# Eight-head attention that sums its second exponentials on TensorE, taps and evictions moved to ScalarE, and strands ranked by arrival

## The chip, the cores and the metric

The kernel runs on one core of one Trainium2 chip. The metric is the device time of one execution in microseconds (us); the time before is the median of three executions. A core has five engines with a queue of their own each: TensorE (PE, matmuls, with its weight loads shown apart as PEld), VectorE (DVE), ScalarE (ACT), GpSimd (POOL) and SyncE (SP), which here only issues DMA transfers. Matmul results land in PSUM, eight banks of 128 partitions by 512 float32; everything else is in SBUF or in device memory.

## The reference

Eight images of 256 channels by 32 x 32 points (N = 1024 positions) go through four layers. Only the parts that matter here are shown.

```
layer 0   four-head attention + 3x3 depthwise position term, then a gated feed-forward:
          1x1 conv to 1024 channels, 3x3 depthwise conv, gelu(x1) * x2, 1x1 conv, 8x8 FFT filter
layer 1   xn = group_norm(x)
          q, k, v = 8 heads of 32 channels from one 1x1 conv
          attn = softmax(q^T k * temperature, over keys)       # 1024 x 1024 for each head
          out = v attn^T ;  x = x + w_out out + b_out ;  then a small MLP
layer 2   quantized bottleneck: 1x1, 3x3, 1x1 conv
layer 3   Mamba over four scan orders: in-projection, causal conv of 4 taps + SiLU, selective scan
          with 16 states, gate, out-projection
```

## The kernel before, in words

The program has two phases, one after the other on the same core.

`phase_a` holds layers 0 to 2 and the in-projection and causal conv of layer 3 (`mix`). `phase_b` holds the selective scan. The change touches `phase_a` alone.

In `phase_a` the work of each image is written as a Python generator, a strand, that yields instructions. `sample(b)` runs `layer0`, `feed_forward`, `layer1`, `layer2` for image `b` and then adds the strand `mix(b)`. Image `b` may begin when image `b - 3` is through layer 0, so some three images are on their way at once. A planner, the class `_Order`, writes the instructions out: it keeps a planned time for each engine and buffer from fixed costs in `_Op`, and emits next the strand whose next instruction can start earliest; ties go to the lower rank, a pair of (class, image), and among equal ranks to the strand that was added first. So the order on every engine is fixed when the program is built. The planner also fills gaps on TensorE with dummy matmuls of a constant (`keep_dense`, line 302), where less than half of its last 3.4 us was dense work in its own plan.

Buffers are rooms of numbered tiles. PSUM is the room `bank` with 8 banks. While an attention runs (`attending` is a lock, one attention at a time), all other strands together may hold `OTHERS` = 3 banks; the attention holds one accumulator `po` and takes 4 banks for each step of scores.

Attention goes over the scores twice:

- `maxima` (line 620): for each of 8 position tiles, 2 key halves and 4 heads it makes a 128 x 512 block of scores, VectorE takes its maximum (`tensor_reduce`, 128 x 512 from PSUM), and ScalarE makes the exponentials of that block with `accum_out`, the sum along the row. The bank goes back after that. From maxima and sums a short chain of small operations makes the logarithm of the softmax denominator, which is written as three bfloat16 terms in rows (`parts`, `rows`). `MAXIMA` is the number of strands that share one such list.
- `exponentials` (line 686): for each key tile it makes four transposed blocks of scores, adds minus those rows by a bfloat16 matmul, takes the exponentials on ScalarE (`exps`), and multiplies them with v on TensorE into `po` (`values`). Since the rows hold the whole log-denominator, the result is already normalised; `finish` only copies `po` out.

One image has 64 blocks of maxima and 16 steps in layer 0, and 128 blocks (two groups of four heads) and 32 steps in layer 1. In layer 1 a `finish` ends 8 steps, four times for each image.

Other places that the change touches: the first tap of the depthwise conv in `feed_forward` (`chunk`, 8 of 128 x 1024 for each image, VectorE), the eviction of `k` in `layer1` (4 of 128 x 512 for each image, VectorE), and in `mix` the eviction of the in-projection (8 of 128 x 512, VectorE) and the first tap with its bias of the causal conv (16 of 128 x 1024, VectorE; the other three taps follow on VectorE, then SiLU on ScalarE). `mixing` is a lock: one image is mixed at a time.

Nearly all instructions are emitted by one helper, so the profile puts them on line 154; tiles tell them apart.

Of the kernel before, what the change touches and what calls it, by code (L numbers as in the profile page):

```python
# [344 lines left out]
def phase_a(ctx, tc, i, col, ident, codes, w_parts, mixes):  # L345
# [20 lines left out]
    OTHERS = 3  # L366
    MAXIMA, SCORES = 1, 1.29
    GATE = 1
# [5 lines left out]
    mixing = []  # L374
    RANK = lambda b: (2, b)
    stats = _Room(rooms, "stats", 3, [P, 2, 2, NT, 4])
# [30 lines left out]
    mean = const("mean", [P, P], 1.0 / C)  # L407
    minus = const("minus", [P, P], -1.0, BF16)
    eps0 = const("eps0", [P, 1], 1e-6)
    parts = const("parts", [P, NT, 4, 32], 0.0)  # L410
# [208 lines left out]

    def maxima(rank, q, k, rows, done):  # L620

        both = yield from take(stats)
        least, sums = both[:, 0], both[:, 1]
        todo = [(t, j, h) for t in range(NT) for j in range(2) for h in range(4)]
        left = [MAXIMA]

        def some():
            while todo:
                yield lambda: not todo or may(min(3, len(todo)))
                if not todo:  # L630
                    break
                n = min(len(todo), 4)
                while not may(n):
                    n -= 1
                n = min(n, 4)
                take_now, todo[:n] = todo[:n], []
                bb = yield from some_banks(n)
                ops = []
                for b, (t, j, h) in zip(bb, take_now):
                    r = slice(32 * h, 32 * h + 32)  # L640
                    ops.append(T.matmul(b, lhsT=q[r, t * P : (t + 1) * P], rhs=k[r, hs(j)], start=True, stop=True))
                yield (0.96 if n > 2 else 1.06, ops)
                for b, (t, j, h) in zip(bb, take_now):
                    m, s = (x[:, j, t, h : h + 1] for x in (least, sums))
                    yield V.tensor_reduce(m, b, AX.X, ALU.max, negate=True)
                    yield A.activation(b, b, AF.Exp, bias=m, accum_out=s)
                    back(b)
            left[0] -= 1

        for _ in range(MAXIMA):  # L650
            order.add((1, rank), some())
        yield lambda: left[0] == 0 and not making
        making.append(1)
        m, mx, t = (small.tile([P, NT, 4], F32, name=f"mx{e}", tag=f"mx{e}", bufs=2) for e in range(3))
        yield V.tensor_tensor(m, least[:, 0], least[:, 1], ALU.min)
        for j in range(2):
            yield V.tensor_tensor(least[:, j], m, least[:, j], ALU.subtract)
        yield A.activation(least, least, AF.Exp)
        yield V.tensor_tensor(sums, sums, least, ALU.mult)
        yield V.tensor_tensor(t, sums[:, 0], sums[:, 1], ALU.add)  # L660

        y = small.tile([P, NT, 4], F32, name="ln", tag="ln", bufs=2)
        put(stats, both)
        yield A.activation(y, t, AF.Ln)
        yield V.tensor_tensor(mx, y, m, ALU.subtract)
        yield A.activation(y, y, AF.Exp, scale=-1.0)
        yield V.tensor_tensor(t, t, y, ALU.mult)
        yield V.scalar_tensor_tensor(mx, t, -1.0, mx, ALU.add, ALU.add)
        for e in range(2):
            b = small.tile([P, NT, 4], BF16, name="mb", tag="mb", bufs=2)  # L670
            yield V.tensor_copy(b, mx)
            yield V.tensor_copy(parts[:, :, :, e], b)
            yield V.tensor_tensor(mx, mx, parts[:, :, :, e], ALU.subtract)
        yield V.tensor_copy(parts[:, :, :, 2], mx)
        for h in range(2):
            pr = yield from side()
            yield [
                T.transpose(pr[:, t * P : (t + 1) * P], parts[:, 4 * h + t].rearrange("p a b -> p (a b)"), ident)
                for t in range(4)
            ]  # L680
            yield A.copy(rows[:, hs(h)], pr)
            back(pr)
        making.clear()
        done()

    def exponentials(rank, tasks, vt, n, finish):

# [4 lines left out]
        for task, (h, steps) in enumerate(tasks):  # L692
            po = yield from take(bank)
            seen = [0]

# [27 lines left out]

            def values(k, four, tiles, po=po, seen=seen, last=len(steps) - 1):
                es = [t[:, e] for t in tiles for e in range(2)]
                yield lambda: seen[0] == k
                ops = []
                for e, (q, kk, rows, key, r, c, at) in zip(es, four):
# [5 lines left out]
                    )  # L734
                yield (0.88 * (4 * n // P) + 0.12, ops)
                for t in tiles:
                    put(exps, t)
# [4 lines left out]
            yield lambda: seen[0] == len(steps)  # L742
            order.add((0, rank), finish(task, po))
        attending.clear()
# [17 lines left out]
    def layer0(b, x):  # L762
        rank = b
        xn = yield from rms(x, "n1w", "n1b")
# [47 lines left out]

        def finish(task, po):
            h, p = divmod(task, 2)
# [52 lines left out]
    def feed_forward(b, x):  # L867


        rank = b  # L870
        xn = yield from rms(x, "n2w", "n2b")
# [8 lines left out]
        def chunk(o):  # L880
# [19 lines left out]

            yield V.tensor_scalar(acc, hx, w(4), None, ALU.mult)
            for k, dy, dx in _taps():
# [80 lines left out]
    def layer1(b, x):  # L983
        rank = b
        xn = yield from group_norm(x, "g1", "be1")
# [7 lines left out]
        for cc in range(CC):  # L993
            for n in range(2):
                ws.append((yield from weights("w_qkv1", CC * n + cc)))
            for n, dst in enumerate((q, k)):
                w = ws.pop(0)
                for h in range(2):
                    ps = yield from side()
                    yield mm(ps, w, 0, P, xn, h)  # L1000
                    if n == 0:
                        yield A.activation(dst[:, cc, hs(h)], ps, AF.Identity, scale=temp[:, cc : cc + 1])
                    else:
                        yield V.tensor_copy(dst[:, cc, hs(h)], ps)
                    back(ps)
                put(wr, w)
# [3 lines left out]

            order.add((1, rank), maxima(rank, q[:, cc], k[:, cc], rows[cc], done))
        for cc in range(CC):
# [12 lines left out]
        for g in range(CC):  # L1025

            def finish(h, po, g=g):
                yield A.copy(o[:, g, hs(h)], po)
                put(bank, po)
                summed[0] += 1  # L1030

# [7 lines left out]
            yield lambda g=g: ready[g]  # L1039
            yield from exponentials(rank, [(h, steps) for h in range(2)], vt, HD1, finish)  # L1040
            put(low, rows[g])
# [122 lines left out]
    def mix(b):  # L1164


        def branch(c, k, src, back, left):
# [4 lines left out]

            yield V.tensor_scalar(o, src, col("cv_w", 4 * c + PAD), col("cv_b", c), ALU.mult, ALU.add)
            for tap in range(PAD):
# [15 lines left out]
        def chunk(c):  # L1190
# [5 lines left out]
            for h in range(2):  # L1196
# [7 lines left out]
                put(low, xc)  # L1204
                yield V.tensor_scalar(xi[:, hs(h)], ps, col("s3"), None, ALU.mult)
                back(ps)
# [36 lines left out]
    with tc.manual_schedule():  # L1243
        for b in range(B):
            order.add((2, b), sample(b))
        order.add((9, B), weight_parts())
# [604 lines left out]
```

## Time and profile before

| | |
|---|---|
| median of 3 executions | 9355.51 us (9354.29 to 9357.71) |
| profiled execution, its own time | 9359.27 us |
| its span in the profile | 9357.5 us |
| granted TensorE clock, mean | 0.98 |
| last write of `mix`, end of the work of `phase_a` | about 3773 us |
| first scan of `phase_b` | 3807 us |

The span is the time from the first to the last instruction of the program in the profiled execution. Busy time of an engine is the time in which one of its instructions is shown as running; for TensorE the ends are modelled, so that a matmul that is held up by a bank counts as busy. A group is all instructions of one operation on tiles of one name.

### The profile page before, as it was taken

To read this page: it belongs to the slowest core of one execution; us is meant where nothing else is said; L and a number is where in the kernel's file an instruction comes from. 1 tells how busy PE (TensorE), PEld (TensorE's weight loads), DVE (VectorE), ACT (ScalarE), POOL (GpSimd) and SP (SyncE) were. 2 spreads that over 40 slices of the span, in tenths; PEclk is the share of its full clock that TensorE was granted. 3 is DMA by queue.
4 is the path that set the end of the run, shared out by engine and by line. 5 is a ranking of instruction groups with operands and counts; after the bars stand their busy time and mean duration, and the time that the engine had idled before them with its cause. 6 is when DMAs were issued, how large, how long until landed. Compare 5 with 4: busy or idle time off the path is not lost.

```text
span 9357.5 us, 152821 instructions
## 1 busy us (share of the span) xinstructions
PE 8721.1 (93%) x56752; PEld 5778.5 (62%) x56752; DVE 8236.6 (88%) x9134; ACT 7996.2 (85%) x15039; POOL 5674.9 (61%) x2742
## 2 busy tenths in 40 slices
PE   9999999999999998799999999999999999999998
PEld 3333333333333333688788788778788788787787
DVE  7688587969899777899999999999999999999898
ACT  7768576767777774899999999999999999999998
POOL 0010010101111100799999999999999999999999
PEclk9999999999999999999999999999999999999999
DMA  1100111111111112222222212212222222222221
GB/s 57 38 25 22 38 55 49 48 35 49 34 64 57 39 52 85 76 64 66 69 65 66 73 61 65 73 61 67 71 62 68 69 67 65 68 67 64 69 66 58
DMA packets 297420, 548.41 MB, mean 59 GB/s; under 512 B 31761, under 2 KB 98705, under 8 KB 291554
## 3 DMA queue, kind: packets, MB, share of 16 engines
q1 hardware_dynamic: 296674, 538.64, 17.8%
q8 instruction: 446, 7.31, 0.3%
q14 instruction: 300, 2.46, 0.1%
HBM read 427.90 MB, written 100.14 MB: 56 GB/s over the span
## 4 chain that ended last, share of the span: by engine, by line
ACT 24%; PE 24%; DVE 16%; issue 3%; POOL 1%; DMA 0%; DVEq 0%; SPq 0%; POOLq 0%; ACTq 0%
ACT da L154 11%; DVE h L154 11%; ACT dbu L154 9%; PE db L154 8%; PE py L154 7%; PE pp L154 5%; PE bank L154 3%; DVE mx L154 1%; DVE mid L154 1%; DVE stats L154 1%; DVE ys L154 1%; ACT dt L154 1%; ACT L154 1%; DVE yT L154 1%; ACT st L154 1%
## 5 line engine op out<-in xcount | busy, mean ns | idle before, releaser
L154 POOL TENSOR_TENSOR h<-h,cb 128x1024 f32<-128x1024 f32 x2048 | 4798.5, 2388 | 144.2 <-ACT st L154 79.8
L154 ACT ACTIVATE da<-dt,am 128x512 f32<-128x512 f32 x4096 | 2867.8, 714 | 138.5 <-DVE h L154 130.7
L154 DVE TENSOR_TENSOR_SCAN h<-da,db 128x512 f32<-128x512 f32 x2048 | 2330.3, 1199 | 227.9 <-PE db L154 132.2
L154 DVE TENSOR_TENSOR_SCAN h<-da,st,db 128x512 f32<-128x512 f32 x2048 | 2444.0, 1258 | 68.1 <-PE db L154 47.3
L154 ACT ACTIVATE dbu<-du,bT 128x512 f32<-128x512 f32 x3584 | 2476.9, 708 | 9.3 <-PE db L154 5.0
L154 PE MATMUL db<-ident,dbu 128*128 128x128 f32 x14336 | 2134.6, 277 | 316.0 <-DVE h L154 303.6
L154 PE MATMUL py<-ident,h 128*128 128x128 f32 x16384 | 2121.5, 273 | 10.4 <-POOL h L154 6.5
L154 PEld LDWEIGHTS db<-ident,dbu 128*128 128x128 f32 x14336 | 1614.4, 141 | 748.0 <-DVE h L154 486.2
L154 PEld LDWEIGHTS py<-ident,h 128*128 128x128 f32 x16384 | 1849.9, 140 | 29.9 <-POOL h L154 10.6
L154 ACT ACTIVATE bank<-bank,stats 128x512 f32<-128x512 f32 x1536 | 1018.8, 676 | 369.8 <-DVE stats L154 362.8
L154 DVE TENSOR_REDUCE stats<-bank 128x1 f32<-128x512 f32 x1536 | 976.4, 680 | 222.0 <-PE bank L154 218.0
L154 ACT ACTIVATE exps<-bank 128x512 f32<-128x512 f32 x1536 | 793.8, 612 | 194.7 <-PE bank L154 189.6
L154 PE MATMUL bank<-big,big 32*128 32x512 f32 x4096 | 873.8, 659 | 40.7 <-ACT bank L154 18.2
L154 DVE SCALAR_TENSOR_TENSOR mid<-mid,cols,mid 128x961 f32<-128x961 f32 (+2 forms) x560 | 726.0, 1296 | 12.5
L154 POOL COPY mx<-mx 128x1024 f32<-128x1024 f32 x28 | 64.4, 2301 | 903.6 <-DMA mix<-mx 534.9
L154 PEld LDWEIGHTS bank<-big,big 32*128 32x128 f32 x4096 | 297.5, 190 | 480.0 <-issue 209.9
L302 PE MATMUL bank<-minus 128*128 128x512 bf16 x1994 | 522.5, 404 | 37.7 <-ACT exps L154 17.5
L154 PE MATMUL db<-dg,du 128*128 128x128 f32 x4096 | 530.4, 279 | 17.0 <-DVE h L154 16.1
L154 PE MATMUL bank<-exps,big 128*32 128x512 f32 (+1 forms) x3072 | 538.7, 611 | 0.0
L154 POOL TENSOR_TENSOR mid<-mid,mid 128x512 f32<-128x512 f32 x64 | 102.6, 1623 | 689.8 <-DVE mid L154 630.4
L154 PEld LDWEIGHTS db<-dg,du 128*128 128x128 f32 x4096 | 488.7, 192 | 49.3 <-DVE h L154 26.3
L302 PEld LDWEIGHTS <-minus 128*128 128x128 bf16 x2080 | 197.4, 102 | 491.9 <-issue 294.3
(204 smaller groups left out, 9271.5 us busy)
## 6 DMA issues: line engine op xcount, KB each, us to landing
cb<-c_d SPq DMA_DIRECT2D x1024, 256.0 KB, 3.2
xs<-mix SPq DMA_DIRECT2D x256, 256.0 KB, 4.3
mix<-mx SPq DMA_DIRECT2D x112, 512.0 KB, 3.0
big<-in_x_dram SPq DMA_DIRECT2D x16, 1024.0 KB, 5.3
kept<-big SPq DMA_DIRECT2D x16, 1024.0 KB, 5.2
big<-kept SPq DMA_DIRECT2D x16, 1024.0 KB, 6.9
low<-codes SPq DMA_DIRECT2D x64, 256.0 KB, 3.7
wi<-w_in SPq DMA_DIRECT2D x64, 192.0 KB, 3.4
```

The lines of the kernel that those rows point to most:

```text
L154: return getattr(getattr(nc, self.engine), self.method)(*self.args, **self.kw)
L302: self.nc.tensor.matmul(x, lhsT=self.minus, rhs=rhs, start=True, stop=True)
```

## The change

1. In layer 1, `maxima` is called with `shift=True`: VectorE takes the maxima of the blocks as before, but the exponentials with their sums and the chain that makes the logarithm are left out; the three bfloat16 rows hold the maximum alone. Layer 0 stays as it is.
2. In layer 1, `exponentials` is called with `shifted=True`: it takes a second accumulator bank `pz` and adds to each step four more matmuls, a 128 x 32 block of ones against the same exponentials, so that `pz` holds the denominators. `finish` takes the reciprocal of `pz` on VectorE (128 x 512), multiplies `po` by it on VectorE, and gives both banks back; the copy on ScalarE is gone.
3. The first tap of `feed_forward`'s depthwise conv, the first tap of `mix`'s causal conv, the eviction of `k`, and the eviction of the in-projection go from VectorE to ScalarE.
4. `MAXIMA` goes from 1 to 2, and the image leaves the ranks: all images have rank 0, so that ties go to the strand that was added first.

```diff
-    MAXIMA, SCORES = 1, 1.29
+    MAXIMA, SCORES = 2, 1.29
...
-    RANK = lambda b: (2, b)
+    RANK = lambda b: (2, 0)
...
+    ones = const("ones", [P, HD0], 1.0)
...
-    def maxima(rank, q, k, rows, done):
+    def maxima(rank, q, k, rows, done, shift=False):
...
-                    yield V.tensor_reduce(m, b, AX.X, ALU.max, negate=True)
-                    yield A.activation(b, b, AF.Exp, bias=m, accum_out=s)
+                    yield V.tensor_reduce(m, b, AX.X, ALU.max, negate=not shift)
+                    if not shift:
+                        yield A.activation(b, b, AF.Exp, bias=m, accum_out=s)
                     back(b)
...
+        if shift:
+            yield V.tensor_tensor(mx, least[:, 0], least[:, 1], ALU.max)
+            put(stats, both)
+        else:
+            yield V.tensor_tensor(m, least[:, 0], least[:, 1], ALU.min)
...
+            yield V.scalar_tensor_tensor(mx, t, -1.0, mx, ALU.add, ALU.add)
...
-    def exponentials(rank, tasks, vt, n, finish):
+    def exponentials(rank, tasks, vt, n, finish, shifted=False):
...
             po = yield from take(bank)
+            pz = (yield from take(bank)) if shifted else None
...
+                if shifted:
+                    ops = [
+                        T.matmul(
+                            pz[at : at + n], lhsT=ones[:, :n], rhs=e,
+                            start=(k == 0 and key == 0), stop=(k == last), skip_group_check=True,
+                        )
+                        for e, (_, _, _, key, _, _, at) in zip(es, four)
+                    ]
+                    yield (0.88 * (4 * n // P) + 0.12, ops)
...
-            yield V.tensor_scalar(acc, hx, w(4), None, ALU.mult)
+            yield A.activation(acc, hx, AF.Identity, scale=w(4))
...
-                        yield V.tensor_copy(dst[:, cc, hs(h)], ps)
+                        yield A.copy(dst[:, cc, hs(h)], ps)
...
-            def finish(h, po, g=g):
-                yield A.copy(o[:, g, hs(h)], po)
+            def finish(h, po, pz, g=g):
+                t = yield from take(low)
+                yield V.reciprocal(t, pz)
+                put(bank, pz)
+                yield V.tensor_tensor(o[:, g, hs(h)], po, t, ALU.mult)
                 put(bank, po)
+                put(low, t)
...
-            yield V.tensor_scalar(o, src, col("cv_w", 4 * c + PAD), col("cv_b", c), ALU.mult, ALU.add)
+            yield A.activation(o, src, AF.Identity, scale=col("cv_w", 4 * c + PAD), bias=col("cv_b", c))
...
-                yield V.tensor_scalar(xi[:, hs(h)], ps, col("s3"), None, ALU.mult)
+                yield A.activation(xi[:, hs(h)], ps, AF.Identity, scale=col("s3"))
...
-            order.add((2, b), sample(b))
+            order.add((2, 0), sample(b))
```

`rank = b` becomes `rank = 0` in `layer0`, `feed_forward` and `layer1` as well.

More of the change, by code (lines that the diff above doesn't have):

```diff
@@ L654, in maxima @@
         m, mx, t = (small.tile([P, NT, 4], F32, name=f"mx{e}", tag=f"mx{e}", bufs=2) for e in range(3))
[L655 to L668, printed above, removed]
+        if shift:
[3 more added lines that the diff above has]
+            yield V.tensor_tensor(m, least[:, 0], least[:, 1], ALU.min)
+            for j in range(2):
+                yield V.tensor_tensor(least[:, j], m, least[:, j], ALU.subtract)
+            yield A.activation(least, least, AF.Exp)
+            yield V.tensor_tensor(sums, sums, least, ALU.mult)
+            yield V.tensor_tensor(t, sums[:, 0], sums[:, 1], ALU.add)
+            y = small.tile([P, NT, 4], F32, name="ln", tag="ln", bufs=2)
+            put(stats, both)
+            yield A.activation(y, t, AF.Ln)
+            yield V.tensor_tensor(mx, y, m, ALU.subtract)
+            yield A.activation(y, y, AF.Exp, scale=-1.0)
+            yield V.tensor_tensor(t, t, y, ALU.mult)
+            yield V.scalar_tensor_tensor(mx, t, -1.0, mx, ALU.add, ALU.add)
         for e in range(2):
@@ L722, in step, with values @@
                 order.add((1, rank), values(k, four, tiles))
-            def values(k, four, tiles, po=po, seen=seen, last=len(steps) - 1):
+            def values(k, four, tiles, po=po, pz=pz, seen=seen, last=len(steps) - 1):
                 es = [t[:, e] for t in tiles for e in range(2)]
@@ L742, in exponentials @@
             yield lambda: seen[0] == len(steps)
-            order.add((0, rank), finish(task, po))
+            order.add((0, rank), finish(task, po, pz))
         attending.clear()
@@ L762, in layer0 @@
     def layer0(b, x):
-        rank = b
+        rank = 0
         xn = yield from rms(x, "n1w", "n1b")
@@ L811, in layer0, with finish @@
         summed = [0]
-        def finish(task, po):
+        def finish(task, po, pz):
             h, p = divmod(task, 2)
@@ L867, in feed_forward @@
     def feed_forward(b, x):
-        rank = b
+        rank = 0
         xn = yield from rms(x, "n2w", "n2b")
@@ L983, in layer1 @@
     def layer1(b, x):
-        rank = b
+        rank = 0
         xn = yield from group_norm(x, "g1", "be1")
@@ L1009, in done @@
                 ready[cc] = 1
-            order.add((1, rank), maxima(rank, q[:, cc], k[:, cc], rows[cc], done))
+            order.add((1, rank), maxima(rank, q[:, cc], k[:, cc], rows[cc], done, True))
         for cc in range(CC):
@@ L1039, in layer1 @@
             yield lambda g=g: ready[g]
-            yield from exponentials(rank, [(h, steps) for h in range(2)], vt, HD1, finish)
+            yield from exponentials(rank, [(h, steps) for h in range(2)], vt, HD1, finish, True)
             put(low, rows[g])
```

## The prediction

> **What bounds the kernel now.** I read the page first (engine shares and the slices), then busy time by stretches, the groups by shape, and the waits.
>
> ```profile
> PE 8721.1 (93%) x56752; PEld 5778.5 (62%) x56752; DVE 8236.6 (88%) x9134; ACT 7996.2 (85%) x15039; POOL 5674.9 (61%) x2742
> ...
> PE   9999999999999998799999999999999999999998
> ...
> DVE  7688587969899777899999999999999999999898
> ACT  7768576767777774899999999999999999999998
> ```
>
> The slices show two programs: up to slice 16 VectorE and ScalarE change between 4 and 9, after it all are full. The change touches only the first, `phase_a`, which ends at about 3773 us. Its busy times (columns: stretch, its length, then PE, PEld, DVE, ACT, POOL busy, clock, DMA share, GB/s):
>
> ```profile
> 0.00:3773.00 3773.00, 3513.92 (x16346) 1321.74 (x16346) 2998.82 (x4141) 2662.56 (x5707) 359.91 (x236) 0.95 0.14 47
> 3773.00:9357.50 5584.50, 5207.21 (x40406) 4456.71 (x40406) 5237.77 (x4993) 5333.60 (x9333) 5315.04 (x2506) 1.00 0.21 66
> ```
>
> So the second stretch, 5584.5 us, stays. In the first VectorE is busy 79%, ScalarE 71%, TensorE 93%, but that 93% holds dummies and matmuls held up at a bank. No engine bounds all of it; stretches of 100 us tell which bounds where:
>
> ```profile
> 900.00:1000.00 100.00, 97.20 (x693) 31.85 (x694) 27.14 (x55) 83.80 (x182) 2.52 (x2) 0.97 0.00 1
> ...
> 1100.00:1200.00 100.00, 92.45 (x312) 34.59 (x310) 98.66 (x134) 84.84 (x194) 5.52 (x2) 0.91 0.15 56
> ...
> 1900.00:2000.00 100.00, 98.93 (x554) 44.68 (x549) 48.86 (x97) 76.28 (x183) 3.03 (x4) 1.00 0.00 1
> ```
>
> and the same stretches for the dummies of line 302 alone:
>
> ```profile
> 900.00:1000.00 100.00, 1.38 (x4) 0.97 0.00 1
> ...
> 1100.00:1200.00 100.00, 18.70 (x67) 0.91 0.15 56
> ...
> 1900.00:2000.00 100.00, 0.78 (x2) 1.00 0.00 1
> ```
>
> Two kinds. In 14 of the 38 stretches VectorE is above 90% (1100 is one) and TensorE has up to 27 us of dummies to give: VectorE bounds. In six others (300, 600, 900, 1400, 1900, 3200) there are at most 8 dummies and TensorE is at 94 to 100%: mostly attention, where TensorE bounds. ScalarE is never the fullest of the three in either kind.
>
> The rows that price the change:
>
> ```profile
> L154 ACT ACTIVATE bank<-bank,stats 128x512 f32<-128x512 f32 x1536 | 1018.8, 676 | 369.8 <-DVE stats L154 362.8 <-DVE rs L154 3.1 <-ACT bank L154 0.2
> ...
> L154 ACT ACTIVATION_READ_ACCUMULATOR bank<-bank,stats 128x1 f32 x1536 | 333.2, 217 | 0.0
> ```
>
> ```profile
> L154 PE MATMUL bank<-exps,big 128*32 128x512 f32 x2048 | 288.6, 611 | 0.0
> ```
>
> ```profile
> L154 DVE TENSOR_SCALAR mx<-mx,cols 128x1024 f32<-128x1024 f32 x112 | 92.5, 826 | 20.9 <-POOL mx L154 19.2 <-issue 0.4
> ...
> L154 DVE TENSOR_SCALAR mid<-mid,cols 128x1024 f32<-128x1024 f32 x96 | 82.5, 859 | 37.7 <-ACT mid L154 34.4 <-POOL mid L154 2.7
> ```
>
> ```profile
> PEld bank L154 <- ACT bank L154: 262.0, 400, 5.3
> ...
> PEld bank L154 <- ACT exps L154: 135.4, 282, 2.4
> ```
>
> The first two say what one block of first-pass exponentials costs ScalarE; the third prices the new matmuls (same shape, same 1024 instructions, two records each); then the moved taps; the last two how long TensorE's weight loads waited for banks held by first-pass and by second-pass exponentials.
>
> **The change part by part.**
>
> *Load moved.* ScalarE loses 1024 of 1536 blocks at 0.88 us (1018.8 + 333.2 over 1536), 901 us, and some 12 us of the small chain. It gains 64 first taps of the depthwise conv at 1.05 to 1.27 us (the 128x1024 rows without and with two scalar columns, 1049 and 1271 ns), 75; 128 first taps of `mix` at 1.27, 163; 64 evictions at 0.69, 44; 32 copies of `k` replace 32 copies of `po`. Net -631: 2032 us left, 54%. That covers all it gains, and the saved ScalarE time by itself is worth nothing, since ScalarE bounded no stretch. If the cover were gone, it would be 282 us of new work.
>
> VectorE loses 92.5 (112 taps), 69 (80 of the 96 `mid` taps at 0.859), 41.7 + 5.8 (64 evictions), 21.8 (`k`), and 27 of the small chain: 257. It gains 32 multiplies at 0.69, 22, and 32 reciprocals.
>
> *The reciprocal* has one row, 128x7 at the very start:
>
> ```profile
> 2.81 0.70 DVE L154 TENSOR_SCALAR rs<-cols 128x8 f32<-128x8 f32 x1 [2.81 <-DMA cols<-in_cols_dram]
> ...
> 2.96 0.56 DVE L458 RECIPROCAL rq<-cols 128x7 f32<-128x7 f32 x1
> 3.58 0.45 DVE L481 TENSOR_SCALAR sq<-cols,rq 128x1 f32<-128x1 f32 x2
> ```
>
> The instruction two before it ends at 3.51 and its reader begins at 3.58. At the most 0.07 us are its own, 10 ns an element, 5.1 us for 512. At the least it costs what VectorE's 128x512 copy from PSUM does, 0.69. Dependent small operations here follow each other after some 0.03 us; less that, and less the two elements between, about 0.03 us for 7 remain, 4 ns an element. I take 2.2 us: 32 of them 70 us, between 22 and 163.
>
> The Trainium skill speaks against the change here: "VectorE: DVE Perf Modes", section "First, the fixed hardware budget", says that the reciprocal is an iterative divide with a repeat count of 8. At its 0.96 GHz that is an estimated 4.3 us for 512 elements; the one row neither confirms nor excludes it. By the page 32 times 2.1 us come on top, of which 27% and half of the rest count (steps 1 and 4): 42 us, and the sum would end at about 9308 us.
>
> *Step 1, VectorE-bound stretches.* By the start times of the rows, 56% of `mix`'s taps, 46% of the `mid` taps, 59% of the evictions and 56% of the `k` copies lie in the 14 stretches: 52 + 32 + 28 + 12, and 12 of the small chain, 136 us. Of layer 1's 256 steps 27% lie there; of the new 92 us that puts 25 back. Net -111. Next late there is TensorE, whose 91 to 99% hold dummies. The three later taps now wait for ScalarE; behind them in VectorE's queue stands what the planner has put there, and in the 14 stretches other strands fill it. I take 0; the present waits of VectorE for `mid` from ScalarE are 34.4 us in 7 times, so up to 34.
>
> *Step 2, banks of the first pass.* A layer 1 bank goes back after the maximum instead of after 0.88 us more on ScalarE. Two thirds of the 262.0 us are layer 1's, 175; 56% of the maxima lie outside the 14 stretches: -98 (bounds 0 and -175). Next late is the maximum itself, 0.68 us a block.
>
> *Step 3, sums on TensorE.* 256 steps get four matmuls more, side by side in column groups: measured from each start to the next one's they take 272 us in all, 1.06 a step. 88 steps lie in the six stretches without dummies: +93. The other 168 (179 us) are covered by dummies and VectorE-bound time; the built order has 1174 dummies where there were 1994, 215 us less at 0.262. If that cover is gone, the 179 come on top.
>
> *Step 4, ends of groups.* `finish` holds two banks for 2.2 + 0.69 us where a copy took 0.59: 2.3 later, 32 times, 74 us. The next group's accumulators wait for them, other strands do not; 73% lie outside the 14 stretches, half of that on the path: +27 (0 to 130).
>
> *Step 5, one bank less.* Accumulators and four score banks leave 2 banks instead of 3. Layer 1's share of the waits for second-pass exponentials is two thirds of 135.4, 90 us, 0.35 a step; the new 1.06 a step lies over it. I take 0, up to +90.
>
> *Step 6, two maxima strands, order by arrival, the end.* No row shows these. Two strands could take at the best layer 0's third of the bank waits, -87; an image's `mix` that slips past the last image's layer 2 costs 16 branches, 76 us. The built order has 108 of 128 `mix` writes before the last image's last code write, 112 before: four branches more at the end, some 3.9 us each on VectorE, against 0.8 saved on each of 16 or more. +16 and -13: I take 0. SP issues as many DMAs as before; GpSimd gets three instructions more.
>
> *Sum.* -111 - 98 + 93 + 27 = -89, on the profiled execution's 9359.3: 9270. That execution is 4 above the median of the runs, so 9355.5 - 89 = **9266 us**.
>
> **The rivals.**
> 1. *TensorE becomes the bound (slower).* For it: 93% busy and +272. Against: 820 dummies fewer. It costs the 179 us of step 3: -89 + 179 = +90, 9446. It decides once more than 89 of the 179 are uncovered.
> 2. *All overlaps as well as now.* Busy sums are 2999 + 2663 + 3514 = 9176 in 3773, 2.43 engines at once. After: 2834 + 2032 + 3571 = 8437, over 2.43 is 3469: -300, 9055. For it: three fuller engines come nearer to each other. Against: TensorE's share of it cannot shrink to less than its busy 3571.
> 3. *Step 2 is hidden anyway.* For it: ScalarE itself waited 362.8 us for maxima, so the maximum, not the exponential, is late. Then -89 + 98 = +9, 9365, no change that can be told; with half of it, 9315.
>
> **How the numbers follow.** Chances: forecast 0.42 (9200 to 9335), rival 1 0.24, rival 2 or most of the way to it 0.18, rival 3 0.16, of which 0.09 is within 0.2% (19 us, about what this measurement tells from no change), 0.05 above and 0.02 below it. Faster 0.42 + 0.18 + 0.02 = 0.62; same 0.09; slower 0.24 + 0.05 = 0.29. The range leaves out the far part of rivals 1 and 2 and the bounds that would have to fall together: 9140 to 9440; the forecast's own is 9200 to 9335.
>
> **What would show it.** First tap groups of VectorE gone and its stretches above 90% fewer; `PEld bank <- ACT bank` near 90; a `bank<-exps,ones` group near 290 us; the 128x512 reciprocal's mean (above 4 us step 4 and step 1 are too good). The first codes write of the last image and the end of `mix` give each step's sum. The prediction is wrong if TensorE is at 97% or more throughout `phase_a`, or if `phase_b` is not 5584 us.

## The result and the profile after

The changed kernel takes 9336.66 us (median of 17 runs, 9326.52 to 9352.71) where the kernel before takes 9362.99 us in the same comparison (17 runs, 9354.29 to 9370.69). The ratio is 0.9974, with a 95% interval of 0.9966 to 0.9981: 26 us faster, where the forecast was 89. The profiled execution took 9336.66 us.

The page of the changed kernel, engine totals and slices:

```profile
PE 8742.0 (94%) x57896; PEld 5762.6 (62%) x57980; DVE 8141.6 (87%) x8796; ACT 7539.9 (81%) x13201; POOL 5691.1 (61%) x2745
...
DVE  7587688877878976899999999999999999999898
ACT  8774376564445546899999999999999999999998
```

The slices of `phase_a` (up to slice 16) show where work went: in nine of the 16 slices ScalarE's digits fell, in seven of them from 7 to 4 or 5; VectorE's are nearly what they were. The two stretches, cut where the last row of `mix` is written (3751.1 us; it was 3773.1):

```profile
0.00:3754.00 3754.00, 3536.88 (x17535) 1305.58 (x17574) 2903.72 (x3803) 2207.32 (x3871) 378.74 (x240) 0.96 0.14 47
3754.00:9334.90 5580.90, 5205.12 (x40361) 4456.99 (x40406) 5237.86 (x4993) 5332.57 (x9331) 5312.34 (x2506) 1.00 0.23 66
```

From the first scan to the end it is 5549.6 us (5550.5 before): `phase_b` is untouched, and all of the difference lies in `phase_a`. There ScalarE is 455 us less busy, VectorE only 95 less and TensorE 23 more. The groups by shape that the change made or moved:

```profile
L302 PE MATMUL bank<-minus 128*128 128x512 bf16 x1174 | 325.7, 410 | 23.9 <-DVE low L154 7.9 <-DVE big L154 5.3 <-ACT low L154 3.1
...
L154 PE MATMUL bank<-exps,ones 128*32 128x512 f32 x2048 | 288.3, 601 | 0.0
...
L154 DVE SCALAR_TENSOR_TENSOR mx<-mx,cols,mx 128x1021 f32<-128x1021 f32 x112 | 144.6, 1292 | 124.3 <-ACT mx L154 124.3
...
L154 ACT ACTIVATE mx<-mx,cols 128x1024 f32<-128x1024 f32 x112 | 136.4, 1246 | 10.2 <-POOL mx L154 9.3
...
L154 DVE RECIPROCAL low<-bank 128x512 f32<-128x512 f32 x32 | 107.3, 3354 | 82.6 <-PE bank L154 77.5 <-issue 3.7 <-POOL big L154 1.4
```

The new matmuls have the price that was forecast. The reciprocal takes 3.35 us. The second tap of `mix` (third line) now idles VectorE for 124.3 us because ScalarE has not made the first tap yet; before, the first tap stood on VectorE itself and no such wait existed. The waits of `phase_a` (engine, what it waited for, then us in total, times, longest):

```profile
ACT big L154 <- PE bank L154: 377.1, 157, 7.7
...
PEld bank L154 <- ACT exps L154: 162.7, 304, 3.0
DVE mx L154 <- ACT mx L154: 124.3, 19, 13.0
PEld bank L154 <- DVE stats L154: 96.9, 174, 3.0
PEld bank L154 <- ACT bank L154: 71.4, 108, 1.7
...
PEld bank L154 <- DVE low L154: 50.2, 29, 5.1
...
PE bank L154 <- DVE low L154: 35.2, 20, 4.3
```

The wait of weight loads for `ACT bank` fell from 262.0 to 71.4, but 96.9 for the maximum (`DVE stats`, 9.7 before) stand in its place. The last two lines are TensorE waiting for VectorE's writes of `low`, nearly all of them the reciprocal, whose end frees a group's second bank. A weight load and its matmul can wait at the same moment; with such time counted once, the two lines are 57 us of idle time, 6 before. ScalarE's idle time is no loss; the first line (135.7 before) says that it now waits for TensorE.

### The profile page after: what moved, and what is told of

Read it like the earlier page. It is cut to its first block, busy times and chain, and to the rows that moved or that the text cites. A ratio compares the mean times of both kernels' runs of the same rounds, so it can differ in the third digit from the quotient of the medians.

```text
span 9334.9 us, 152169 instructions
## 1 busy us (share of the span) xinstructions
PE 8742.0 (94%) x57896; PEld 5762.6 (62%) x57980; DVE 8141.6 (87%) x8796; ACT 7539.9 (81%) x13201; POOL 5691.1 (61%) x2745
## 4 chain that ended last, share of the span: by engine, by line
PE 39%; ACT 26%; DVE 26%; issue 4%; POOL 1%; DMA 0%; DVEq 0%; SPq 0%; POOLq 0%; ACTq 0%
PE bank L154 18%; ACT da L154 12%; DVE h L154 11%; ACT dbu L154 10%; PE db L154 8%; PE py L154 7%; PE pp L154 5%; DVE stats L154 4%; DVE mid L154 4%; DVE mx L154 2%; DVE low L154 1%; DVE big L154 1%; PE bank L302 1%; DVE ys L154 1%; ACT L154 1%
## 5 line engine op out<-in xcount | busy, mean ns | idle before, releaser
L154 DVE TENSOR_REDUCE stats<-bank 128x1 f32<-128x512 f32 x1536 | 952.0, 680 | 198.1 <-PE bank L154 194.6
L154 PE MATMUL bank<-big,big 32*128 32x512 f32 x4096 | 812.1, 662 | 36.6 <-DVE low L154 25.4
L154 PE MATMUL bank<-exps,big 128*32 128x512 f32 (+1 forms) x3072 | 560.7, 620 | 1.0 <-ACT exps L154 1.0
L154 DVE SCALAR_TENSOR_TENSOR mx<-mx,cols,mx 128x1021 f32<-128x1021 f32 x336 | 441.4, 1323 | 130.3 <-ACT mx L154 124.3
L154 ACT ACTIVATE bank<-bank,stats 128x512 f32<-128x512 f32 x512 | 340.2, 687 | 164.8 <-DVE stats L154 163.3
L154 PE MATMUL bank<-big,wr 128*128 128x512 f32 x896 | 450.6, 632 | 13.2 <-POOL big L154 2.9
```

What stands on the lines that cost most here:

```text
L154: return getattr(getattr(nc, self.engine), self.method)(*self.args, **self.kw)
```

## The experiments

Times are medians, ratios are to the kernel before with the 95% interval, and differences in us are between medians. Two kinds of edit must be kept apart. Where the planner sees other work or other costs, it writes a **new order** for all of `phase_a`. Where an order is **held**, the planner plans the kernel as it was, and only the instruction that is emitted differs.

### Parts with a plan of their own

**The attention change alone**: the changed kernel with everything else as before (one strand, ranks by image, the taps and evictions on VectorE).

```diff
-    MAXIMA, SCORES = 2, 1.29
+    MAXIMA, SCORES = 1, 1.29
-    RANK = lambda b: (2, 0)
+    RANK = lambda b: (2, b)
-            yield A.activation(acc, hx, AF.Identity, scale=w(4))
+            yield V.tensor_scalar(acc, hx, w(4), None, ALU.mult)
...
```

> The attention change alone (sums by products of ones, maximum alone in the rows, reciprocal in finish) on the kernel before: taps and evictions stay on VectorE, one maxima strand, image ranks. Theory T (TensorE takes back most of what the banks give): -10 to +60 us against before, since +93 to +272 us of TensorE work meet -98 us of bank waits and VectorE loses only its 27 us of small chain. Theory R (only the slow reciprocal, 32 x 3.35 us, spoils it): -30 to -90 us. Theory O (the new order and ranks spoil it): -60 to -150 us, since the order parts are left out here.

Measured 9550.63 us, ratio 1.0195 (1.0181 to 1.0210): 187 us slower. ScalarE, relieved, waits for TensorE instead: for its exponentials 463.2 us (189.6 before), for `big` 416.3 (135.7 before). The new sums with the reciprocal are no gain by themselves. Which of their costs makes up the 187 no run separates.

**The rest without the attention change**: the changed kernel with layer 1's sums and evictions of `po` as before.

```diff
-            order.add((1, rank), maxima(rank, q[:, cc], k[:, cc], rows[cc], done, True))
+            order.add((1, rank), maxima(rank, q[:, cc], k[:, cc], rows[cc], done))
...
-                yield V.reciprocal(t, pz)
-                put(bank, pz)
-                yield V.tensor_tensor(o[:, g, hs(h)], po, t, ALU.mult)
+                yield A.copy(o[:, g, hs(h)], po)
...
```

> Taps and evictions on ScalarE, two maxima strands, ranks by arrival; the eight-head attention as before. Theory T: -60 to -110 us against before, the relief of the VectorE-bound stretches without the new TensorE work, so faster than the whole change. Theory R: -80 to -120 us. Theory O: 0 to +60 us. If ScalarE, which here keeps its 901 us of first-pass exponentials and gains 282 us, becomes the bound: 0 to +50 us.

9292.75 us, 0.9926 (0.9913 to 0.9938): 44 us faster than the changed kernel, with all of its ScalarE work back. Alone, the two parts are 187 slower and 71 faster; together they are 26 faster. Parts that each get a plan of their own do not add up.

**The taps and evictions alone**: the kernel before with these lines of the changed one.

```diff
-            yield V.tensor_scalar(acc, hx, w(4), None, ALU.mult)
+            yield A.activation(acc, hx, AF.Identity, scale=w(4))
...
-                        yield V.tensor_copy(dst[:, cc, hs(h)], ps)
+                        yield A.copy(dst[:, cc, hs(h)], ps)
...
```

> The kernel before with the taps and evictions on ScalarE alone: attention, one maxima strand and image ranks as before. The taps, the evictions and the order together gave -71 us. Theory W (the relief of VectorE is what pays): -50 to -120 us against before. Theory O (the order pays, the taps only move work to a ScalarE that is full there): 0 to +60 us.

9347.27 us, 0.9980 (0.9971 to 0.9989): 19 us for VectorE work that the forecast held for 136 us on the path, and between the two theories. The first 3700 us of this kernel:

```profile
0.00:3700.00 3700.00, 3492.51 (x16149) 1312.72 (x16150) 2727.41 (x3821) 2874.91 (x5950) 344.29 (x230) 0.96 0.14 46
```

and of the kernel before:

```profile
0.00:3700.00 3700.00, 3482.10 (x16201) 1307.66 (x16202) 2928.35 (x4083) 2629.86 (x5679) 352.37 (x233) 0.96 0.13 46
```

Of the same 3700 us VectorE is 201 us less busy, so 201 longer idle. Its waits in the kernel with the taps moved (before, the first two were 218.0 and 193.1, and there was no wait of the third kind):

```profile
DVE stats L154 <- PE bank L154: 302.9, 111, 20.9
DVE big L154 <- PE bank L154: 292.1, 65, 35.1
DVE mx L154 <- ACT mx L154: 107.5, 19, 17.6
```

There are 85 + 99 us more of waits for TensorE's banks, and 107.5 for ScalarE's first taps: the freed time, and more, became waits of these three kinds.

**The order alone**: the kernel before with two strands and ranks by arrival.

```diff
-    MAXIMA, SCORES = 1, 1.29
+    MAXIMA, SCORES = 2, 1.29
-    RANK = lambda b: (2, b)
+    RANK = lambda b: (2, 0)
...
```

> The kernel before with two maxima strands and ranks by arrival alone. Theory W: -20 to +30 us against before. Theory O: -60 to -120 us.

9305.95 us, 0.9937 (0.9923 to 0.9950): 61 us faster, where Step 6 took 0. And **two strands alone**, the first of these lines without the ranks:

> The kernel before with one number changed: two strands for the maxima in place of one; ranks by image as before. Both changes of order together gave -60 us. If the two strands carry it: -40 to -70 us. If the ranks by arrival carry it (they were worth 36 us in the changed kernel): -10 to -30 us here. If they only work together: within 10 us of before.

9320.88 us, 0.9956 (0.9944 to 0.9969): 40 us.

### Single costs, the order held

**The sums' matmuls left out**: in the changed kernel, held, the four products with ones of steps 1 to 7 of each group are not issued, so the denominators hold one step of eight.

```diff
-                            start=(k == 0 and key == 0), stop=(k == last), skip_group_check=True,
+                            start=(k == 0 and key == 0), stop=True, skip_group_check=True,
...
+                    if k > 0:
+                        for op in ops:
+                            op.method = None
                     yield (0.88 * (4 * n // P) + 0.12, ops)
...
```

> The changed kernel, its planned order held, but the products of ones of steps 1 to 7 of each group of 8 are planned and not issued (the denominators then hold the first key tile alone; that part of the computation is left out). 224 of 256 steps lose some 1.05 us of TensorE. Theory T: -80 to -200 us against the changed kernel. Theory R or O: 0 to -40 us, since TensorE had dummies and idle time to cover them.

9274.68 us, 0.9906 (0.9893 to 0.9920): 62 us less than the changed kernel, between the two expectations. The first 3700 us here, and then in the changed kernel:

```profile
0.00:3700.00 3700.00, 3450.16 (x15784) 1283.43 (x15785) 2902.94 (x3804) 2206.12 (x3871) 377.01 (x242) 0.94 0.14 48
```

```profile
0.00:3700.00 3700.00, 3518.51 (x17460) 1297.81 (x17499) 2859.65 (x3771) 2166.29 (x3834) 373.75 (x237) 0.96 0.14 46
```

The 256 steps' products take some 270 us from start to start, so 7/8 of them are 236; a quarter of that (62) came back. For all of them that is an estimated 71 us. But the granted clock, the number after GpSimd's, fell with them from 0.96 to 0.94. If all 3700 us were matmuls at that clock, this would cost some 74 us, an upper estimate. So the products may cost more than 71 at an equal clock; no run holds the clock.

**A copy in the reciprocal's place**, held: `t` is `pz` itself, so the output is multiplied by the sums where it should be divided by them.

```diff
-                yield V.reciprocal(t, pz)
+                r = V.reciprocal(t, pz)
+                r.method = "tensor_copy"
+                yield r
```

> The changed kernel, its planned order held, with a copy of 128x512 from PSUM (0.69 us) in the place of each of the 32 reciprocals (3.35 us), so the division is left out. VectorE loses 85 us. Theory R: -50 to -85 us against the changed kernel. Theory T or O: 0 to -30 us.

9250.87 us, 0.9880 (0.9866 to 0.9893): 86 us less than the changed kernel. The copy's group in this kernel:

```profile
L154 DVE COPY low<-bank 128x512 f32<-128x512 f32 x32 | 22.0, 686 | 81.6 <-PE bank L154 76.5 <-issue 3.7 <-POOL big L154 1.4
```

The chain of work that ended last, followed back through the first 3754 us, in the changed kernel and then here, as shares of these 3754 us (the lines end where the view ends):

```profile
by line: PE bank L154 45.4%; DVE stats L154 10.3%; DVE mid L154 8.8%; DVE mx L154 4.9%; DVE low L154 3.5%; issue 3.1%; DVE big L154 2.1%; PE bank L302 1.9%; ACT exps L154 1.3%; ACT mx L154 1.0%; ACT mid L154 0.8%; ACT L163 0.7%; POOL big L1
```

```profile
by line: PE bank L154 45.4%; DVE stats L154 11.1%; DVE mid L154 8.6%; DVE mx L154 4.3%; issue 2.7%; DVE big L154 2.1%; PE bank L302 1.7%; DVE low L154 1.5%; ACT exps L154 1.3%; ACT mx L154 1.2%; ACT mid L154 1.0%; ACT L163 0.8%; DVE bn L154
```

32 instructions became 2.67 us shorter, 85 us, and the kernel 86. In the chain VectorE's work on `low`, where the reciprocal stands, fell from 3.5% to 1.5%, from 131 to 56 us: 75 of the 86. TensorE's idle time for `low`, counted once, fell from 57 to 16 us, which shows 41 of it. So what the reciprocal takes beyond a copy is on the path nearly whole.

**Layer 1's first-pass exponentials cut to 128x1**, the kernel before, held; the row sums then hold one column.

```diff
-                    yield A.activation(b, b, AF.Exp, bias=m, accum_out=s)
+                    a = A.activation(b, b, AF.Exp, bias=m, accum_out=s)
+                    if cut:
+                        a.args = (b[:, :1], b[:, :1], AF.Exp)
+                    yield a
...
```

> The kernel before, its planned order held, with the first-pass exponentials of layer 1 cut to one column (128x1 in place of 128x512; the sums of 1024 blocks are then wrong, so that part is left out). ScalarE loses some 660 us and each bank comes back about 0.6 us earlier, nothing else changes. If the bank waits of step 2 were on the path: -70 to -175 us against before. If they were hidden (rival 3 of the prediction): 0 to -30 us.

9355.15 us, 0.9993 (0.9984 to 1.0002): 8 us, or nothing. The groups of this kernel show that the cut is half a cut: 237 ns and the read of the sum stay. (The helper's line 154 is 155 here, and 156 and 157 in the next experiment.)

```profile
L155 ACT ACTIVATION_READ_ACCUMULATOR bank<-bank,stats 128x1 f32 x1536 | 323.1, 210 | 0.3
...
L155 ACT ACTIVATE bank<-bank,stats 128x1 f32<-128x1 f32 x1024 | 242.2, 237 | 563.3 <-DVE stats L155 556.1 <-DVE rs L155 5.4 <-DVE mx L155 0.3
```

```profile
ACT bank L155 <- DVE stats L155: 677.9, 1009, 6.1
...
PEld bank L155 <- ACT bank L155: 246.9, 382, 4.0
```

Still, 0.44 us less by the rows in each of 1024 blocks, 0.36 by ScalarE's busy time (2629.9 to 2261.9 in 3700 us), took only 15 us from TensorE's wait (262.0 before) and lengthened ScalarE's wait for the maxima from 362.8 to 677.9 us. In the order of before it is the maximum that comes late, not the exponential.

**The taps and evictions emitted on ScalarE in VectorE's places**, the kernel before, held. Each moved line is changed like this one:

```diff
-            yield V.tensor_scalar(acc, hx, w(4), None, ALU.mult)
+            r = V.tensor_scalar(acc, hx, w(4), None, ALU.mult)
+            r.real = ((acc, hx, AF.Identity), dict(scale=w(4)))
+            yield r
```

> The kernel before with its order held to the instruction; only the first taps of the depthwise conv and of the mix and the evictions of codes and inner inputs are issued on ScalarE in the place where VectorE did them (the copy of k too where it is the same line; nothing of the attention's sums). The planner does not know of it. Alone and with a plan of its own this move gave -19 us. Theory (VectorE's freed time turns into waits for ScalarE, whatever the order): between -40 and +40 us against before, with a new group of waits of VectorE for the accumulators mx from ScalarE of over 100 us. Rival (the relief is real, 100 us or more, and the new plan spent it): -80 us or more with the order held.

9405.12 us, 1.0051 (1.0038 to 1.0063): 44 us slower, just past the theory's end and far from the rival. VectorE's waits for the moved taps in this kernel:

```profile
DVE mx L157 <- ACT mx L156: 199.4, 73, 17.1
...
DVE mid L157 <- ACT mid L156: 141.3, 45, 19.4
```

The two waits, 341 us against 34.4 before, take more than the forecast's whole relief. The granted clock of the first 3700 us is 0.95 here, 0.96 before, which may be a part of the 44 (an estimate stands below, under the draw); a relief of 100 us is excluded with it or without it. A plan that knows of the move lowers the two waits to 107.5 and 67.9, no further.

### The changed kernel with one thing otherwise

**1/z as exp(-ln z)** on ScalarE, which is idle enough:

```diff
-                yield V.reciprocal(t, pz)
+                yield A.activation(t, pz, AF.Ln)
                 put(bank, pz)
+                yield A.activation(t, t, AF.Exp, scale=-1.0)
```

> The changed kernel with the reciprocal made on ScalarE as exp(-ln z), two activations of 128x512 (some 0.7 and 0.6 us) in place of 3.35 us on VectorE; the planner plans it anew. VectorE loses 107 us, ScalarE gains 42. If VectorE's time is on the path, as the copy in its place showed (-86 us): -50 to -100 us against the changed kernel. If the new order eats it: -20 to +20 us.

9281.87 us, 0.9916 (0.9903 to 0.9930): 55 us less than the changed kernel, and faster than both. **The same with the taps and evictions back on VectorE**:

```diff
-            yield A.activation(acc, hx, AF.Identity, scale=w(4))
+            yield V.tensor_scalar(acc, hx, w(4), None, ALU.mult)
...
```

> The changed kernel with 1/z as exp(-ln z) on ScalarE, and with the first taps and evictions back on VectorE: the new sums and the new order without the move of the taps. With the taps on ScalarE this form stood at about -79 us against before. If the move of the taps is worth its 13 to 19 us also here: -60 us. If its worth is VectorE's 136 us of busy time once the reciprocal no longer stands there: +20 to +50 us against before. If the taps on ScalarE now hurt: below -90 us.

9358.29 us, 0.9997 (0.9988 to 1.0006). By this pair the move is worth 76 us beside the new sums; without them it was 19 alone and 13 on top of the new order (9305.95 and 9292.75). Against before it came out at -3, between the expectation's -60 and its +20 to +50.

**One strand**:

```diff
-    MAXIMA, SCORES = 2, 1.29
+    MAXIMA, SCORES = 1, 1.29
```

> The changed kernel with one maxima strand instead of two. The attention change alone, with one strand and image ranks, was 187 us slower than before. If the single strand is what cost there (it waits for four maxima before it asks for banks again, and has no exponentials to go on with): +80 to +200 us against the changed kernel. If it is the ranks or the taps: -20 to +40 us.

9403.83 us, 1.0043 (1.0031 to 1.0056): 67 us more than the changed kernel, between the two expectations. **Ranks by image**:

```diff
-    RANK = lambda b: (2, 0)
+    RANK = lambda b: (2, b)
...
```

> The changed kernel with the image back in the ranks, two maxima strands. If the ranks are what cost in the attention change alone: +80 to +200 us against the changed kernel. If not: -30 to +40 us.

9372.35 us, 1.0008 (0.9999 to 1.0017): 36 us more.

**No denominators at all**: the changed kernel without the products with ones, the second bank, the reciprocal and the multiply; `po` is copied, and layer 1's attention is not divided by its sums.

```diff
-                t = yield from take(low)
-                yield V.reciprocal(t, pz)
-                put(bank, pz)
-                yield V.tensor_tensor(o[:, g, hs(h)], po, t, ALU.mult)
+                yield A.copy(o[:, g, hs(h)], po)
...
-            yield from exponentials(rank, [(h, steps) for h in range(2)], vt, HD1, finish, True)
+            yield from exponentials(rank, [(h, steps) for h in range(2)], vt, HD1, finish)
```

> The changed kernel without the denominators: the rows hold the maxima alone, but there is no second accumulator, no product of ones, no reciprocal, and finish copies as before (the division by the sums is left out of layer 1); planned anew. Against the kernel with only taps, evictions and order (9293 us) it tells what leaving out 901 us of first-pass exponentials gives when the planner may use it; against the changed kernel it tells what the sums cost. If the first pass is hidden even so: 9270 to 9295 us. If the new order uses it: 9120 to 9220 us.

9153.07 us, 0.9776 (0.9762 to 0.9789): 184 us less than the changed kernel, and 140 less than the kernel with the taps and order but the old attention (9292.75), which differs from it by the 1024 first-pass blocks and their chain.

**The new sums for one of the two groups of heads only**, with exp(-ln z):

```diff
-            order.add((1, rank), maxima(rank, q[:, cc], k[:, cc], rows[cc], done, True))
+            order.add((1, rank), maxima(rank, q[:, cc], k[:, cc], rows[cc], done, cc == 0))
...
             def finish(h, po, pz, g=g):
+                if pz is None:
+                    yield A.copy(o[:, g, hs(h)], po)
...
```

> A candidate: the new sums for one of layer 1's two groups of heads only, with exp(-ln z) on ScalarE for the reciprocal; the other group as before. TensorE gets half of the products of ones (136 us), ScalarE loses half of the exponentials (450 us). If TensorE and the single engines share the bound: 9230 to 9270 us, faster than 9282 (all groups, exp(-ln z)) and 9293 (none). If the order decides: 9270 to 9320 us.

9278.04 us, 0.9907 (0.9894 to 0.9921): faster than both kernels, and the same as exp(-ln z) for both groups.

### The draw of the order

How much of such differences is the order that the planner happened to write? The planner's cost of one step of score products (`SCORES`) was moved by 0.01; the work stays the same but for the dummies (8796 instructions of VectorE and 13201 of ScalarE in all three draws of the changed kernel).

```diff
-    MAXIMA, SCORES = 2, 1.29
+    MAXIMA, SCORES = 2, 1.30
```

> The changed kernel with the planner's cost of a score product put at 1.30 in place of 1.29, nothing else: the same work in a newly drawn order. It gauges how far any new plan of the same work scatters. If the terms of some 30 us are terms of the mechanism: within 15 us of the changed kernel. If the planner's order scatters by more than these terms: 20 to 60 us off, to either side.

9398.68 us, 1.0044 (1.0031 to 1.0056): 62 us more than the changed kernel with 1.29. The same edit of the kernel before:

> The kernel before with the planner's cost of a score product put at 1.30 in place of 1.29, nothing else: the same work in a newly drawn order. The same edit of the changed kernel cost it 62 us. If a newly drawn order scatters by so much in any kernel: 20 to 60 us off, to either side, and the 26 us between the two kernels are then within what the draw gives. If only the changed kernel, where ranks follow the arrival, is that sensitive: within 15 us of before.

9383.86 us, 1.0024 (1.0014 to 1.0034): 23 us more. And 1.28 in the changed kernel:

> The changed kernel with the planner's cost of a score product put at 1.28 in place of 1.29, nothing else: a third draw of the order for the same work. If the order on record is a usual draw: within 40 us of it to either side. If it is a lucky one and the draw at 1.30 the usual: +30 to +80 us against it, so that the change would by itself be slower than before. If the draw at 1.30 is the unlucky one: within 15 us of it or below it.

9400.03 us, 1.0040 (1.0027 to 1.0052): 63 us more. The last write of `mix` is at 3819.0 and 3803.7 us in the two draws of the changed kernel (3751.1 on record), and from the first scan to the end it is 5549.5 and 5549.3: the draw, too, acts in `phase_a` alone. The granted clock of the first 3700 us is 0.95 in these two draws and 0.96 in the one on record; in both draws of the kernel before it is 0.96. If all 3751 us were matmuls at that clock, 0.01 would be an estimated 38 us, so the clock may carry a part of the 62 and 63, and none of the 23. No run separates it from the waits.

So three draws of the changed kernel stand at 9337, 9399 and 9400, two of the kernel before at 9361 and 9384. About their means (9378 and 9372) they lie with a standard deviation of some 30 us, by 3 degrees of freedom; a difference of two single draws has then some 43. The 26 us are real for the two programs as they stand, but five draws do not show that the change, apart from its draw, gains or loses anything. Of the comparisons with plans of their own, the attention change alone (+187) and the sums as a whole (184) are well beyond the draw, and leaving out the first pass (140) by less; the order (61), the rest without the attention (44 against the changed kernel), exp(-ln z) (55), the taps (13 to 76), the strands (40 and 67) and the ranks (36) are not, one by one.

## Why the prediction was right and wrong

**Sign and range** held for the two programs as they stand; the size did not, by 63 us. By the draws the sign is luck: the changed kernel's other two orders (9399 and 9400) are slower than either order of the kernel before (9361 and 9384).

*Load moved*: its cover held, but its sizes were too large. ScalarE lost 455 us of busy time, not 631. The step added an exponential's row and the row of its read (0.88 us), but the two run partly at once: counted once they cover 1104.8 us for the 1536 blocks of the kernel before, 0.72 each. 1024 such blocks less the 282 us gained are the 455. Nothing followed from it, since ScalarE bounded no stretch of the kernel before.

*The reciprocal* is the step that failed most clearly. Taken 2.2 us, measured 3.35, inside the bounds 0.69 to 5.1. The repeat count of 8 that the Trainium skill's page "VectorE: DVE Perf Modes", section "First, the fixed hardware budget", names had given an estimated 4.3: too long, but it pointed the right way, and 3.35 lies about midway between that and the value taken. Worse than the size was the share: of what the reciprocal takes beyond a copy, Steps 1 and 4 put 31 us on the path (13 as 27% of 32 times 1.51, and 18 as 27 times 1.51 over 2.3). The copy in its place showed 86, nearly all of it in the chain. *Step 4* had named the place, the banks that a group's end holds, but had said that other strands do not wait for them, and had taken half to be hidden. They do wait. TensorE's order is fixed, and in the changed kernel a product of another strand, with weights `wr`, stands still behind a reciprocal:

```profile
1184.94 3.35 DVE L154 RECIPROCAL low<-bank 128x512 f32<-128x512 f32 x1
...
1188.35 0.50 PEld L154 LDWEIGHTS bank<-big,wr 128*128 128x128 f32 x2 [3.27 <-DVE low L154]
1188.35 3.53 PE L154 MATMUL bank<-big,wr 128*128 128x512 f32 x4 [2.56 <-DVE low L154]
```

These two lines of TensorE are also one wait seen twice, as a weight load's and as a matmul's.

*Step 1*, -111. The mechanism failed, not only a size. VectorE's stretches above 90% did become fewer, 9 of 38 for 14, but the time it was freed of turned into waits for ScalarE's first taps and for TensorE's banks. The sentence "in the 14 stretches other strands fill it. I take 0" is the false one: with the order held the new waits ate the relief, and the kernel became 44 us slower, at a granted clock of 0.95 for 0.96; a plan of its own gave -19. (TensorE was at 86 to 99% in the 14 stretches, not at 91 to 99.) The bound that went with it, 34 us from the wait for `mid`, was too low: 124.3 for `mx` and 65.0 for `mid`. That VectorE is full over a stretch says that much of its work is ready there; it does not say that the stretch ends sooner when a tenth of that work goes to an engine that must hand it back in the middle of a chain.

*Step 2*, -98. The line `PEld bank <- ACT bank` fell to 71.4 (forecast near 90), but half of it came back as the maximum's 96.9, which the step named as next late and did not price. Rival 3's reading of the 362.8 us holds for the order of before as far as a half cut can tell: cutting half of the exponential there gave 8 us. With a plan of its own, leaving out the whole first pass gave 140, which is beyond the draw but not by much. Between these the step's 98 stays unsettled; that half the exponential earns next to nothing with the order held is shown.

*Step 3*, +93: some 270 us of TensorE time against 272, and 71 on the path by the held run, at a lower clock. Most of the rest stayed covered (dummies 522.5 to 325.7 us), so rival 1's 9446 fell: of the 236 us taken out, 62 came back. *Step 5*: waits for second-pass exponentials rose by 27, from 135.4 to 162.7, between the 0 taken and the 90 of its bound.

*Step 6*, 0 with -87 to +76, had bounds that held and too little weight. Two strands and ranks by arrival alone gave -61, and a new draw of the same work moves the time by up to 63 us. The forecast treated the order as a term; it is the error of every other term.

**The sum.** If the two held runs add, they put 86 + 71 = 157 us on the reciprocal's excess and the sums' matmuls, where the forecast had 31 + 93 = 124: 33 of the missing 63 us. The other 30 are gains that came out at 183 instead of 213; that is less than the draw, and no run here says which step lost them. Rival 2 was far off: busy sums are 3537 + 2904 + 2207 = 8648 in 3754 us, 2.30 engines at once, fewer than the 2.43 of before.

## What to carry to other kernels

When a planner writes the order, first move one of its costs by a hundredth and measure how far the same work scatters: a forecast or a verdict below that is about the draw, and only edits with the order held price a single instruction. The reciprocal that held accumulator banks at the end of each group counted here nearly in full, though VectorE was idle for 850 of the 3754 us; look for all who wait for such an instruction before taking a share of it. Moving the head of a chain to another engine adds a handover per chain, which is to be priced at that engine's queue, not at the instruction.

## What was not expected of the hardware

VectorE's reciprocal of 128x512 from PSUM takes 3354 ns, 4.9 times the copy of the same shape (686), or about 6.5 ns an element with its fixed part. Taking it as exp(-ln z) on ScalarE, whose two instructions take 596 and 631 ns in that kernel (the group of the second holds 32 others of its shape), makes the whole kernel 55 us faster in the one draw measured:

```profile
L154 ACT ACTIVATE low<-low 128x512 f32<-128x512 f32 x64 | 40.4, 631 | 1.9
...
L154 ACT ACTIVATE low<-bank 128x512 f32<-128x512 f32 x32 | 19.1, 596 | 26.5 <-PE bank L154 26.1
```

An exponential with its row sum shrinks far less than its columns do: at 128x1 its row still takes 237 ns and the read's 210, half of the 0.88 us of the two rows at 128x512. The first tap of `mix` takes ScalarE 1246 ns where VectorE took 826, so the move also makes the chain's head half as long again.
